# Two layers on one core: later groups convolve by four shifted products, and the long filter moves ahead of the inverse

## The chip, the core and the metric

The kernel is one program on one core of a Trainium2 chip. The metric is device time in microseconds (us) of one execution; of several runs the median is taken. A core has TensorE (PE; its weight loads are listed as PEld), VectorE (DVE), ScalarE (ACT), GpSimd (POOL) and SyncE (SP, which here issues every DMA). Each engine takes its instructions strictly in the order in which they stand in its queue.

## What is computed

Input x has 2 batches of 1024 rows of 128 features. Four blocks follow each other, each with a residual and a layer norm behind it: softmax attention with 8 heads, a gated feed-forward block with ternary weights (ffn0), a gated delta-rule attention on chunks of 32 rows (here L1), and a feed-forward block with weights of plus and minus one (ffn1). The change touches L1:

```python
q = silu(causal_dwconv(x @ Wq, conv_q))      # 4 taps, per channel; k and v alike
beta = sigmoid(x @ Wb)
q, k = l2norm(q), l2norm(k)                  # per head, in chunks of 32 rows
A = (k * beta) @ k.T
T = inv(eye + tril(A, -1))
u, w = T @ (v * beta), T @ (k * beta)
# scan over the chunks, state S of 32x32 per head
u_i = u_i - w_i @ S
o_i = q_i @ S + tril(q_i @ k_i.T) @ u_i
S = S + k_i.T @ u_i
local_short = causal_dwconv(v, fir_short)    # 3 taps
local_long = causal_dwconv(v, fir_long)      # 31 taps
o = w_global * o + (1 - w_global) * (p0 * v + p1 * local_short + p2 * local_long)
out = rmsnorm(o) @ Wo
```

## The kernel before

The 2048 rows are cut into four groups of 512 (`GROUPS`, line 60): 0 and 1 are the halves of batch 0, 2 and 3 those of batch 1. Group 1 needs from group 0, and 3 from 2, the last rows of projections and values and the scan's state S (`prev`, line 1443; copies on POOL such as L1122, L1240, L1248, L1406).

Four streams of instructions are written out (`PLAN`, line 54): one does ffn0 of groups 0 to 3 and then ffn1 of groups 0 to 3, on one set of buffers; one does L1 of groups 0 and 2, one L1 of group 1, one L1 of group 3. The attention (`pass1`, `pass2`) is written before all of them. Streams "b" and "c" (groups 1 and 3) are `late`: their buffers lie where the attention's lay, so they begin only after it, and some of their steps are written for DVE and ACT instead of POOL. Their PSUM banks (`BANKS`, line 52) are one for group 1 and two for group 3; the stream of groups 0 and 2 has one and gets a second for group 2.

The order on each engine is not that of the text. A planner in the file (`Plan`, lines 168 to 524) builds the graph of dependencies, gives every instruction a price, and simulates all engines. Among the instructions that are ready it takes the one with the best rank: a backward critical path less a bonus per step and group, from the table `AHEAD` (line 20), in us. `RUN` (line 18) holds three more: `switch` is a penalty for PE changing its tile shape; when PE's real work of the last window is under `target` columns and nothing is ready, the planner puts in a dummy product of constants (tile ip, line 1594, and a small form through L1066). The order found is then fixed by dependencies.

L1 of one group (`l1_attn`, line 1072) has these steps:

- l1prep: transposes of the group's rows into xT (L782, L1100), then `conv` for k. `conv` (line 1103) projects with one product of float32 128x512 (L1106), copies it behind three columns of the half before (ACT L1112, POOL L1109 or L1111), multiplies by the last tap (ACT L1115 in late groups, DVE L1117 in the others), adds three taps on DVE (L1119), takes tanh (ACT L1121); then (th+1)*a on DVE gives k (L1142), q (L1188) or v (L1238).
- l1gate: one product, then the gates; norms of k on POOL (L1131, L1133, a power) and beta (L1165 to L1182). Then `conv` for q.
- l1gram: small products of k with k and q (L1066), scaled by DVE (L1199 needs nbet, L1200).
- l1inv: the inverse of the two 16x16 blocks, 15 steps of two DVE instructions (L1214, L1215), in the tiles `nm` and `pr`; ACT or POOL scales (L1225, L1227), DVE transposes (L1228).
- l1v: `conv` for v, L1238, a transposed copy vC (L1246), products with beta (L1250, L1251).
- l1fir: the short filter on ACT, DVE or POOL; for the long one eight DMAs copy vC into two tiles of tag `pj` (L1277), eight DMAs bring 128 KB each of Toeplitz matrices into the tiles `nm` and `pr` in turn (L1282), and 128 small products follow (L1286), 16 for each of the eight loads; DVE takes the result (L1298). Late groups do this after l1v, groups 0 and 2 after the scan.
- l1T doubles the inverse's blocks (products, L1321, L1325), l1wu forms w, u and the scan's matrices, l1scan does 16 dependent steps (L1398 or L1066, L1401), l1out and l1rms finish (L1425 to L1441).

The tags decide the order of l1inv and l1fir: the matrices of the long filter use `nm` and `pr`, so they can be loaded only when the inverse has let go of them.

In front, `prep_rest` (line 709) splits the weights of ffn0 into two parts each and writes them back to HBM (L714, L718, L719); `norm_in` (line 788) loads one half of x into `xt`, normalises it (DVE for the first, POOL L776 for the second) and transposes it; `proj` fills `hi` and `lo`, which SP copies into the stacks (L862, L869).

The line numbers are those of the profile before.

Of the kernel before, what the change touches and what calls it, by code (L numbers as in the profile page):

```python
# [17 lines left out]
RUN = {'dummies': True, 'target': 4688, 'rewarm': False, 'switch': 282251}  # L18
TURNS = 5
AHEAD = {  # L20
    "ffn0": {"00": 33.9, "01": 19.1, "10": -42.8, "11": -632.3},
    "ffn1": {"00": -414.5, "01": 8.0, "10": 14.7, "11": 14.8},
    "l1T": {"00": -49.6, "01": 20.4, "10": -47.0, "11": -18.8},
    "l1fir": {"00": 34.9, "01": 73.7, "10": -3.2, "11": 151.3},
    "l1gate": {"00": 58.9, "01": 42.1, "10": 2.8, "11": 7.5},
    "l1gram": {"00": 143.6, "01": -110.1, "10": 30.9, "11": 98.4},
    "l1inv": {"00": -57.9, "01": 14.3, "10": 69.3, "11": 4.6},
    "l1out": {"00": -136.2, "01": -72.3, "10": -173.5, "11": 60.6},
    "l1prep": {"00": 13.3, "01": -18.5, "10": 28.2, "11": 119.7},
    "l1rms": {"00": 42.7, "01": -222.7, "10": 82.0, "11": 22.0},  # L30
    "l1scan": {"00": -5.2, "01": 75.8, "10": 102.9, "11": 103.9},
    "l1v": {"00": 34.4, "01": 4.4, "10": 11.7, "11": -8.4},
    "l1wu": {"00": 23.3, "01": -28.3, "10": 20.7, "11": -28.0},
    "norm_in": {"0": 303.2, "1": 23.6},
    "pass1": {"0": 29.5, "1": 252.9, "2": -5.4, "3": -11.7, "4": 23.4, "5": -36.2, "6": 62.4, "7": 23.3},
    "pass2": {"0": -31.7, "1": -116.1, "2": -18.2, "3": 37.7, "4": 31.5, "5": 146.2, "6": 75.2, "7": 6.1},
    "post": {"00": 118.3, "01": 180.9, "10": 872.1, "11": 572.6},
    "prep": {"": 42.3},
    "stacks": {"00": -46.3, "01": 58.4, "10": -93.7, "11": -15.8},
    "stk": {"0": 3.6, "1": -44.0, "2": 10.1, "3": -43.0, "4": -60.5, "5": 0.7, "6": -48.2, "7": -0.5},  # L40
    "weights": {"": 53.1},
}
HALVES, RU = 1, 1
O1, O2, O3, O4 = 0, 1, 1, 1
# [483 lines left out]
def body(ctx: ExitStack, tc: tile.TileContext, A, out, dbg=None):  # L528
# [3 lines left out]
    plan, early, alive = Plan(), set(), []  # L532

# [61 lines left out]
    eye16 = const.tile([128, 16, 16], F32, name="eye16")  # L595
    wd = dram.tile([14, 128, 2, 4, 128], F32R, name="wd")
# [112 lines left out]
    def prep_rest():  # L709

        mark("weights")
        for c in range(11):
            raw = FA.big.tile([128, 512], F32, tag="u", name="raw", bufs=2)
            nc.sync.dma_start(out=raw, in_=A["wf"][c])  # L714
            w = FA.big.tile([128, 2, 4, 128], F32R, tag="w", name="w", bufs=FA.wb)
            hi = w[:, 0].rearrange("p a b -> p (a b)")
            nc.scalar.copy(hi, raw)
            nc.gpsimd.tensor_tensor(w[:, 1].rearrange("p a b -> p (a b)"), raw, hi.bitcast(F32), ALU.subtract)  # L718
            nc.sync.dma_start(out=wd[c].bitcast(F32), in_=w.bitcast(F32))  # L719
# [15 lines left out]
        nc.sync.dma_start(out=eye16, in_=A["eye16"])  # L735
        ku4 = FA.big.tile([128, 7, 128], mybir.dt.uint32, tag="alo", name="ku4", bufs=2)
# [51 lines left out]
    def norm_in(b):  # L788

        mark(f"norm_in:{b}")  # L790
        xt = xp.tile([128, 8, 128], F32, tag="xt", name="xt")
# [168 lines left out]
    def mm3(p, whi, wlo, ahi, alo, nk):  # L960
        for k in range(nk):
            n = 0
            for w, a in ((whi, ahi), (wlo, ahi), (whi, alo)):
                nc.tensor.matmul(p, w(k), a(k), start=(k == 0 and n == 0), stop=(k == nk - 1 and n == 2))  # L964
                n += 1
# [15 lines left out]
    def ffn0(F, gi, late):  # L981
# [22 lines left out]
        for c0, cs in ((2, C_H1S), (6, C_H2S)):  # L1004
            nhi = t2048(F, "ahi")
# [66 lines left out]
    def l1_attn(L, gi, late):  # L1072
# [19 lines left out]
        def m(label):  # L1092
            mark(f"{label}:{b}{hg}")
# [5 lines left out]
        xT = own("xT", (128, 512))  # L1099
        nc.scalar.copy(xT, px)  # L1100
        h3 = halo("h3", (128, 3, 3))

        def conv(w, mi):

            p = bank(L, [128, 512])
            nc.tensor.matmul(p, mats[:, mi, :], xT, start=True, stop=True)  # L1106
            pj = own("pj", (128, 515), 2)
            if first:
                nc.gpsimd.memset(pj[:, 0:3], 0.0)  # L1109
            else:  # L1110
                nc.gpsimd.tensor_copy(pj[:, 0:3], pb["pj"][:, w, :])  # L1111
# [10 lines left out]
            nc.gpsimd.tensor_copy(h3[:, w, :], pj[:, 512:515])  # L1122
# [79 lines left out]
        m("l1inv")  # L1202

        xa = tmp("xa", C3)
        nc.vector.transpose(xa, flat(an).rearrange("p (b e) -> p e b", e=16))
        am = own("am", (128, 16, 16))
        nc.vector.tensor_scalar(am, xa[:, :, 0:16], sc(C_EV), None, ALU.mult)
        nc.vector.scalar_tensor_tensor(am, xa[:, :, 16:32], sc(C_OD), am, ALU.mult, ALU.add)
        nm = own("nm", (128, 16, 16))
        nc.gpsimd.tensor_copy(nm, eye16)  # L1210
        pr = own("pr", (128, 16, 16))
        for k in range(15):
            o = pr[:, 0:15 - k, 0:k + 1]
            nc.vector.tensor_tensor(o, bcast(am[:, k, k + 1:16], k + 1), nm[:, k:k + 1, 0:k + 1].to_broadcast([128, 15 - k, k + 1]), ALU.mult)  # L1214
            nc.vector.tensor_tensor(nm[:, k + 1:16, 0:k + 1], nm[:, k + 1:16, 0:k + 1], o, ALU.add)  # L1215
            if k % 5 == 4:
                yield 4.0
                m("l1inv")
        nB = own("nB", C3)
        tt = own("tt", C3)  # L1220
        for e, src, dst in ((side, nm, tt), (nc.gpsimd, nm.rearrange("p i k -> p k i"), nB)):
            xn = tmp("xn", C3)
            for i, c in ((0, C_EV), (16, C_OD)):
                if late and O3:
                    nc.scalar.activation(xn[:, :, i:i + 16], src, AF.Identity, scale=sc(c))  # L1225
                else:
                    e.tensor_scalar(xn[:, :, i:i + 16], src, sc(c), 0.0, ALU.mult, ALU.add)  # L1227
            nc.vector.transpose(flat(dst).rearrange("p (b e) -> p e b", e=16), xn)  # L1228
        yield 4.0
        m("l1v")  # L1230

        th, a = conv(2, M_LV)
        vT = own("v", (128, 514))
        if first:
            nc.gpsimd.memset(vT[:, 0:2], 0.0)
        else:
            nc.gpsimd.tensor_copy(vT[:, 0:2], pb["v"])
        nc.vector.scalar_tensor_tensor(vT[:, 2:514], th, 1.0, a, ALU.add, ALU.mult)  # L1238
        hv = halo("hv", (128, 2))
        nc.gpsimd.tensor_copy(hv, vT[:, 512:514])  # L1240
        vC = own("vC", (128, 17, 32))
        if first:
            nc.gpsimd.memset(vC[:, 0, :], 0.0)
        else:
            nc.gpsimd.tensor_copy(vC[:, 0, :], pb["vC"])
        nc.vector.transpose(flat(vC[:, 1:17, :]), vT[:, 2:514])  # L1246
        hvC = halo("hvC", (128, 32))
        nc.gpsimd.tensor_copy(hvC, vC[:, 16, :])  # L1248
        kv = own("kv", (128, 16, 64))
        nc.gpsimd.tensor_tensor(kv[:, :, 0:32], kC, bcast(betk, 32), ALU.mult)  # L1250
        side.tensor_tensor(kv[:, :, 32:64], vC[:, 1:17, :], bcast(bet, 32), ALU.mult)  # L1251
        yield 5.0

        def fir():
# [16 lines left out]

            pf = bank(L, [128, 32, 16])
            v2 = [own("pj", C3, 2) for hp in range(2)]
            for h in range(4):
                for j in range(2):
                    o = 64 * (h % 2) + 32 * j
                    nc.sync.dma_start(out=v2[h // 2][o:o + 32], in_=vC[32 * h:32 * h + 32, j:j + 16, :])  # L1277
            row = []
            for d in range(32):
                if d % 4 == 0:  # L1280
                    toep = own(("nm", "pr")[d // 4 % 2], (128, 2, 4, 32))
                    nc.sync.dma_start(out=toep, in_=A["toep"][d // 4])  # L1282
                for h in range(4):
                    g, e = divmod(h, 2)
                    s = slice(64 * e, 64 * e + 64)
                    row.append(nc.tensor.matmul(pf[32 * h:32 * h + 32, d, :], toep[s, g, d % 4, :], v2[g][s, :, d],  # L1286
                                                start=True, stop=True, tile_position=(64 * e, 32 * h)))
                if d % 4 == 3:
                    together(row)
                    row = []  # L1290
                if d == 15:
                    yield 4.0
                    m("l1fir")
            yield 4.0
            m("l1fir")
            nc.gpsimd.tensor_tensor(fsC, fsC, bcast(ge[:, :, 1], 32), ALU.mult)
            lC = own("xT", C3)
# [9 lines left out]
            nc.gpsimd.tensor_tensor(wgl, wgl, rq, ALU.mult)  # L1307
            yield 5.0
            return lC

        if late:
            lC = yield from fir()
            steps = [own("pj", (128, 4, 128), 2) for i in range(2)]
            for st in steps:
                nc.gpsimd.memset(st, 0.0)
# [381 lines left out]
```

## Time and profile before

| what | us |
|---|---|
| median of 3 runs | 618.89 (616.68, 618.89, 622.49) |
| the profiled execution, its own time | 621.76 |
| its span, first to last instruction | 620.0 |
| PE busy, mean granted clock | 572.1, 0.981 |
| DVE, ACT, POOL busy | 422.5, 338.6, 248.0 |
| dummy products on PE (L1594 alone) | 28.7 |
| DMA moved | 57.63 MB, 93 GB/s |

The page gives for each engine busy time, share of the span and instructions; then the span in 40 slices of 15.5 us, each digit the busy share in tenths, and under PEclk the clock that PE was granted. Windows give the same numbers for chosen stretches, for all work or for that of one tile. The chain of waits is followed back from the last instruction, at each step to what released it: "DMA nm<-toep" is a load of filter matrices for which the next product waited, "SPq L1277" the time in which SP issued copies.

The stages of the profiled execution: preparation to about 46 us; attention, with ffn0 of groups 0 and 1 and most of L1 of group 0 between, to 342; the rest of ffn0 (last product at 454.4); L1 of groups 1 to 3; ffn1 of group 0 from 460, of group 1 from 552, of group 2 from 575, of group 3 from 595.

### The profile page before, as it was taken

Reading aid. Unit: us, or ns where it says so; the run is one execution under the profiler, and the core shown is the slowest. Engines: PE = TensorE matmul, PEld = TensorE weight load, DVE = VectorE, ACT = ScalarE, POOL = GpSimd, SP = SyncE. Lnnn points to the kernel's source line nnn. Section 1 sums busy time; section 2 is a strip of 40 time slices with the busy share of each in tenths; the row PEclk is TensorE's granted clock in tenths of the full one; section 3 lists DMA queues with packets and bytes.
Section 4 is the critical chain, followed back from the end, with each engine's and each line's share of the span. In section 5 each row is a group of like instructions: output and inputs, shape, how many; then the busy total and the mean of one; then the engine's idle time right before and its main releaser. Section 6 shows DMA issues by size and latency. Waiting matters only on the chain.

```text
span 620.0 us, 18247 instructions
## 1 busy us (share of the span) xinstructions
PE 572.1 (92%) x7729; PEld 360.7 (58%) x7758; DVE 422.5 (68%) x994; ACT 338.6 (55%) x611; POOL 248.0 (40%) x343
## 2 busy tenths in 40 slices
PE   4889999999999999999999989987989998799984
PEld 2264455567665556666556656664666655567653
DVE  5957888884736799498742266885588788374763
ACT  3676456764868884886887562352444523125331
POOL 6886021221303426023691561567514832561210
PEclk9979999999999999999999999999799999999997
DMA  8697520216131323213112433252313203202220
GB/s 258 202 287 267 121 40 2 42 44 176 45 103 55 65 69 119 69 35 121 29 44 71 129 111 104 89 172 69 136 39 80 80 21 94 68 6 70 86 86 17
DMA packets 26595, 57.63 MB, mean 93 GB/s; under 512 B 4049, under 2 KB 12881, under 8 KB 26514
## 3 DMA queue, kind: packets, MB, share of 16 engines
q1 hardware_dynamic: 26514, 56.47, 30.3%
q8 instruction: 61, 1.00, 0.7%
q14 instruction: 20, 0.16, 0.1%
HBM read 40.40 MB, written 8.39 MB: 79 GB/s over the span
## 4 chain that ended last, share of the span: by engine, by line
PE 70%; DVE 10%; DMA 8%; ACT 5%; issue 3%; POOL 2%; SPq 2%; POOLq 0%; ACTq 0%; DVEq 0%
PE ps L964 17%; PE pv L931 10%; PE s L924 10%; PE ps L884 9%; PE ps L1066 7%; PE ps L1449 3%; PE ps L1450 3%; DMA nm<-toep 3%; DMA raw<-wf 3%; SPq L1277 1%; PE ip L1594 1%; PE ps L1286 1%; DVE cv L1119 1%; PE ps L1106 1%; PE ps L782 1%
## 5 line engine op out<-in xcount | busy, mean ns | idle before, releaser
L886 DVE TENSOR_REDUCE mp<-ps 128x1 f32<-128x512 f32 x224 | 140.4, 682 | 47.6 <-PE ps L884 47.0
L926 ACT ACTIVATE p<-s 128x512 f32<-128x512 f32 x236 | 131.1, 600 | 47.4 <-PE s L924 34.3
L964 PE MATMUL ps<-ahi,w 128*128 128x512 f32 x352 | 124.0, 416 | 2.6 <-ACT u L1017 2.4
L924 PE MATMUL s<-q,k 128*128 128x512 f32 x236 | 92.0, 422 | 0.2 <-ACT p L926 0.2
L884 PE MATMUL ps<-k,q 128*128 128x512 f32 x240 | 87.8, 424 | 2.9 <-DVE m L892 1.1
L964 PEld LDWEIGHTS ps<-ahi,w 128*128 128x128 f32 x352 | 65.1, 192 | 23.8 <-ACT p L926 3.4
L931 PE MATMUL pv<-p,va 128*32 128x512 f32 x512 | 72.0, 601 | 0.0
L964 PE MATMUL ps<-alo,w 128*128 128x512 f32 x176 | 71.7, 408 | 0.2 <-POOL alo L979 0.2
L884 PEld LDWEIGHTS ps<-k,q 128*128 128x128 f32 x240 | 43.8, 190 | 34.8 <-DVE mp L886 17.8
L924 PEld LDWEIGHTS s<-q,k 128*128 128x128 f32 x236 | 42.8, 189 | 25.4 <-ACT p L926 14.4
L1449 PE MATMUL ps<-ahi,w 128*128 128x512 f32 x96 | 39.8, 414 | 2.4 <-DVE alo L1465 2.0
L1001 POOL TENSOR_TENSOR alo<-u,ahi 128x512 fp32r<-128x512 f32 x16 | 20.7, 1291 | 52.4 <-ACT ahi L1000 46.0
L1450 PE MATMUL ps<-alo,w 128*128 128x512 f32 x96 | 39.5, 412 | 1.0 <-DVE alo L1465 0.7
L964 PEld LDWEIGHTS ps<-alo,w 128*128 128x128 f32 x176 | 33.7, 192 | 8.8 <-POOL alo L979 0.8
L1464 ACT ACTIVATE ahi<-ps 128x512 fp32r<-128x512 f32 x32 | 18.7, 597 | 27.8 <-PE ps L1450 27.6
L1119 DVE SCALAR_TENSOR_TENSOR cv<-pj,cvh,cv 128x512 f32<-128x512 f32 x36 | 30.6, 851 | 4.3 <-ACT cv L1115 4.0
L1465 DVE SCALAR_TENSOR_TENSOR alo<-ps,ahi 128x512 fp32r<-128x512 f32 x32 | 21.6, 687 | 16.7 <-ACT ahi L1464 16.6
L1594 PE MATMUL ip<-rest 128*128 128x512 bf16 x110 | 28.7, 379 | 2.4 <-issue 1.9
L931 PEld LDWEIGHTS pv<-p,va 128*32 128x32 f32 x512 | 13.3, 108 | 29.2 <-issue 27.2
L859 POOL MEMSET q<- 2x1024 f32 x5 | 4.8, 950 | 63.2 <-issue 37.0
L1401 DVE TENSOR_TENSOR tt<-ps,an 128x32 f32<-128x32 f32 x64 | 11.7, 185 | 25.6 <-PE ps L1066 19.3
L766 POOL TENSOR_SCALAR r<-mv 128x4 f32<-128x4 f32 (+1 forms) x24 | 6.3, 261 | 44.8 <-DVE mv L764 39.8
(264 smaller groups left out, 1061.9 us busy)
## 6 DMA issues: line engine op xcount, KB each, us to landing
w<-wd SPq DMA_DIRECT2D x56, 512.0 KB, 3.4
wd<-w SPq DMA_DIRECT2D x14, 512.0 KB, 4.2
raw<-wf SPq DMA_DIRECT2D x11, 256.0 KB, 3.1
pr<-toep SPq DMA_DIRECT2D x16, 128.0 KB, 3.0
nm<-toep SPq DMA_DIRECT2D x16, 128.0 KB, 3.1
pj<-vC SPq DMA_DIRECT2D x32, 64.0 KB, 2.0
q<-hi SPq DMA_DIRECT2D x14, 128.0 KB, 2.3
k<-hi SPq DMA_DIRECT2D x28, 64.0 KB, 2.4
```

The lines of the kernel that those rows point to most:

```text
L884: nc.tensor.matmul(p, q[:, s * 128:(s + 1) * 128], d, start=True, stop=True)
L886: nc.vector.tensor_reduce(mp[:, s, e, i:i + 1], p, AX.X, ALU.max)
L924: nc.tensor.matmul(s2, ks[e][:, t * 128:(t + 1) * 128], q[:, i * 512:(i + 1) * 512], start=True, stop=True)
L926: nc.scalar.activation(p, s2, AF.Exp, scale=0.25)
L931: together([nc.tensor.matmul(pv[32 * j:32 * j + 32, :], va[:, t - 1, 2 * pr + j % 2, :], pend[j % len(pend)], start=(t == 1), stop=(t == 8 ...
L964: nc.tensor.matmul(p, w(k), a(k), start=(k == 0 and n == 0), stop=(k == nk - 1 and n == 2))
L1066: r.append(nc.tensor.matmul(p(hs), lhsT(hs), rhs(hs), start=True, stop=True, tile_position=(32 * h, 32 * h)))
L1119: nc.vector.scalar_tensor_tensor(a, pj[:, t:t + 512], cvh[:, 4 * w + t:4 * w + t + 1], a, ALU.mult, ALU.add)
L1449: nc.tensor.matmul(p, w(k), ahi(k), start=(k == 0), stop=False)
L1450: nc.tensor.matmul(p, w(k), alo(k), start=False, stop=(k == nk - 1))
L1465: nc.vector.scalar_tensor_tensor(lo, p, 0.0, hi.bitcast(F32), ALU.max, ALU.subtract)
L1594: order[n] = Op(nc.tensor.matmul(ip, rest[:, 0:128], rest, start=True, stop=True).ins, 0)
```

## The change

For groups 1, 2 and 3 (`CVG = 1`) projection and convolution become four float32 products that accumulate in one bank, each with the weight matrix times one tap (`wc`, made in `prep_rest`: a broadcast load of the taps, one scaling, three multiplies on POOL) and a view of xT shifted by one column. xT gets three columns in front, zero or copied from the half before. Tanh reads the bank, and the step behind reads tanh and the bank. Group 0 convolves as before.

The matrices of the long filter in groups 1 and 3 get a pool of five tiles of their own (`TR = 5`). In these groups l1v and the long filter are written before l1inv (`FE = 1`), and the short filter and the sum stay behind it; the planner still chooses the order.

`xt` shares the buffer of `hi` (`XH = 1`); `mm3` and the split of the weights are the same as before (`ZLO = 0`). ffn0 and ffn1 are marked in three parts each, so that `AHEAD` has more rows; all its numbers are new, `target` goes from 4688 to 3863 and `switch` from 282251 to 95802.

```diff
-RUN = {'dummies': True, 'target': 4688, 'rewarm': False, 'switch': 282251}
+RUN = {'dummies': True, 'target': 3863, 'rewarm': False, 'switch': 95802}
...
-    "l1fir": {"00": 34.9, "01": 73.7, "10": -3.2, "11": 151.3},
-    "l1inv": {"00": -57.9, "01": 14.3, "10": 69.3, "11": 4.6},
-    "l1prep": {"00": 13.3, "01": -18.5, "10": 28.2, "11": 119.7},
+    "l1fir": {"00": 76.3, "01": -58.9, "10": -81.4, "11": -84.8},
+    "l1inv": {"00": 101.8, "01": 124.4, "10": 110.0, "11": 21.8},
+    "l1prep": {"00": 10.8, "01": 11.3, "10": -147.9, "11": -216.2},
...
+ZLO, CVG, XH, TR, FE = 0, 1, 1, 5, 1
...
+        if wc is not None:
+            nc.sync.dma_start(out=wc, in_=A["cw"].to_broadcast([128, 1536]).rearrange("p (w t c) -> p w t c", w=3, t=4))
+            half = FA.big.tile([128, 3, 128], F32, tag="u", name="half", bufs=2)
+            nc.gpsimd.tensor_scalar(half, mats[:, 0:3, :], 0.5, 0.0, ALU.mult, ALU.add)
+            for w in range(3):
+                nc.gpsimd.tensor_tensor(wc[:, w], wc[:, w], half[:, w:w + 1, :].to_broadcast([128, 4, 128]), ALU.mult)
...
-        xt = xp.tile([128, 8, 128], F32, tag="xt", name="xt")
+        xt = xp.tile([128, 8, 128], F32, tag="hi" if XH else "xt", name="xt")
...
-        xT = own("xT", (128, 512))
+        xTh = own("xT", (128, 515))
+        xT = xTh[:, 3:515]
...
         def conv(w, mi):
             p = bank(L, [128, 512])
+            if gi >= CVG:
+                for t in range(4):
+                    nc.tensor.matmul(p, wc[:, w, t, :], xTh[:, t:t + 512], start=t == 0, stop=t == 3)
+                th = tmp("th")
+                nc.scalar.activation(th, p, AF.Tanh)
+                return th, p
...
-                    toep = own(("nm", "pr")[d // 4 % 2], (128, 2, 4, 32))
+                    toep = own(("nm", "pr")[d // 4 % 2], (128, 2, 4, 32)) if tpool is None or gi not in (1, 3) else tpool.tile([128, 2, 4, 32], F32, tag="toep", name="toep", bufs=TR)
...
+        if late and FE:
+            vT, vC, hv, hvC, kv = yield from values_()
+            lC = yield from fir_long()
+            nB, tt = yield from inverse()
+        else:
+            nB, tt = yield from inverse()
+            vT, vC, hv, hvC, kv = yield from values_()
+            lC = None
         if late:
-            lC = yield from fir()
+            lC = yield from fir(lC)
...
+    if TR:
+        tpool = pool("toepp", 1, None, ctx, reuse_waits="tile")
```

## Prediction

> **What bounds the kernel now.** I read the page first: busy shares, the 40 slices with the granted clock, the chain that ended last; then the windows of the stretch after the attention, once for all engines and once for the dummy products alone (tile ip), then the chain and the timeline around group 3.
>
> ```profile
> PE 572.1 (92%) x7729; PEld 360.7 (58%) x7758; DVE 422.5 (68%) x994; ACT 338.6 (55%) x611; POOL 248.0 (40%) x343
> PE   4889999999999999999999989987989998799984
> PEclk9979999999999999999999999999799999999997
> PE 70%; DVE 10%; DMA 8%; ACT 5%; issue 3%; POOL 2%; SPq 2%; POOLq 0%; ACTq 0%; DVEq 0%
> ...
> L1119 DVE SCALAR_TENSOR_TENSOR cv<-pj,cvh,cv 128x512 f32<-128x512 f32 x36 | 30.6, 851 | 4.3 <-ACT cv L1115 4.0
> L1594 PE MATMUL ip<-rest 128*128 128x512 bf16 x110 | 28.7, 379 | 2.4 <-issue 1.9
> ```
>
> TensorE (PE) looks like the bound everywhere, at 92%. But the share mixes two stages, and L1594 is work without use: products of constants that the planner puts in where nothing is ready. Up to 342 us (last attention products) the PE row is full with real work. Behind it:
>
> ```profile
> 342.00:454.00 112.00, 101.36 (x1722) 68.53 (x1723) 70.94 (x163) 48.15 (x79) 59.04 (x83) 0.95 0.36 112
> 454.00:545.00 91.00, 81.67 (x2806) 55.09 (x2822) 67.81 (x196) 30.63 (x64) 41.79 (x59) 1.00 0.23 65
> 545.00:620.00 75.00, 61.41 (x977) 45.19 (x972) 43.13 (x129) 25.27 (x52) 18.00 (x22) 0.96 0.17 54
> ```
> ```profile
> 342.00:454.00 112.00, 8.28 (x52) 0.95 0.36 112
> 454.00:545.00 91.00, 24.00 (x173) 1.00 0.23 65
> 545.00:620.00 75.00, 8.12 (x41) 0.96 0.17 54
> ```
>
> First fence: length, busy PE, weight loads, DVE, ACT, POOL, then granted clock. Second: the part of PE that is dummies. Idle plus dummies is 10.6+8.3=18.9, 9.3+24.0=33.3 and 13.6+8.1=21.7 us: 73.9 of 278 us are free. So after 342 the end is set by a chain, and the chain of waits says which:
>
> ```profile
> 517.17 0.55 DVE cv L1119
> ...
> 522.30 0.58 SPq L1277
> ...
> 527.14 3.31 DMA pj<-vC
> 530.50 0.45 PE ps L1286 x27
> 530.97 3.71 DMA nm<-toep
> 534.72 0.52 PE ps L1286 x33
> 535.24 2.84 DMA nm<-toep
> 538.12 0.52 PE ps L1286 x33
> 538.63 3.08 DMA nm<-toep
> ```
>
> This is the last group (3). Its inverse ends at 517.2 (last transpose, L1228); then value convolution, eight copies of vC, and the long filter in rounds: load two matrices, two short sets of products, load again. No arithmetic engine is the limit here.
>
> **Part 1, one set of shifted products (groups 1, 2, 3; nine convolutions).** Removed: 27 L1119 at 0.851 us = 23.0, and 3 L1117 at 0.745 = 2.2 on DVE; 9 L1112 at 0.591 and 6 L1115 at 0.685 = 9.4 on ACT; some 18 POOL copies and memsets at about 0.2 = 3.6. Added: 27 products. One L1106 product is two records, and the chain prices such a pair at 0.86 us: 23.2 us of PE, 7.7 per group. Their weight loads (0.19 each) run beside PE.
>
> Groups 1 and 2 convolve between 354 and 449: +15.5 us where 18.9 us are free. Two stalls of that stretch should go with Part 3 and the freed DVE. At 421.9-432.0 PE ran 1.9 us of filter products and 4.8 of dummies while ffn0 of group 3 waited; its input was written by DVE L979 at 425.7, its product came at 432.2, behind the filter in PE's order: 6.5 us. Then the clock halves; by its means in 3.4 us windows (the last but two of the columns below) from 432.7 to 442.9, 10.2 us, 5.1 lost:
>
> ```profile
> 426.90:430.30 3.40, 2.25 (x70) 1.29 (x71) 0.30 (x1) 0.00 (x0) 2.93 (x1) 1.00 0.31 80
> 430.30:433.70 3.40, 1.87 (x67) 1.33 (x68) 0.00 (x1) 0.96 (x2) 0.04 (x1) 0.85 0.03 6
> 433.70:437.10 3.40, 3.40 (x15) 2.02 (x15) 3.40 (x7) 1.46 (x4) 2.90 (x6) 0.50 0.82 306
> ```
>
> Net +15.5-6.5-5.1=+4 us; ends -11 (all added work fits the free time) and +15.5 (no stall goes). I take +4: the stretch had only 16% free, nearer to full than to empty.
>
> For group 3 the products are on the path. Its k product started at 475.4 and its gram inputs were complete at 500.5 (L1188): 25.1 us, mostly DVE queueing (the L1119 of q ran at 491.3-494.0, the L1188 waited until 499.2). Now 3.44 for k, 0.86 gate, 3.44 for q, tanh 0.64, L1188 1.04, hand-overs 0.5: 9.9 us. But L1199 also needs nbet, which POOL wrote at 492.1 behind a 2.9 us power; k comes 3.7 us earlier (480.1 instead of 483.8), so 488.4. L1199 moves from 501.8 to 488.4 at best, 13 us. I take -7, half, since scans and ffn1 still hold DVE at 75% in 454-545; ends 0 and -13.
>
> A new wait: the product's bank is now held until th and it are combined, so tanh 0.64 and 0.7 to 1.0 of DVE, instead of two ACT copies (0.59+0.69). Group 1 has one bank; its next product (gate, gram) waits at the head of PE's in-order queue, everything behind it too. About 0.2 to 1.5 us for each of 3; in the ends above.
>
> Group 3 also waited for its input: L776 began at 464.7, the other three ran at 471.8, behind group 2's convolution and value work. 3.0 us of it vanish: -2 (0 to -7).
>
> **Part 2, preparation and buffers in front.** A broadcast load of 768 KB: 512 KB took 3.4 us, 448 KB 6.5, so 5 to 10 us of queue q1; on POOL one scale (0.69 for 128x512, L1267) and three multiplies (1.32, L718): 4.6 us. All in the first 60 us, where DMA runs at 0.97 in 40-50. It delays the copies wd<-w; their first readers are the L969 at 57.4 and L964 at 120.4, so 60 us of cover: 0, or +5 to +10 if it weren't there. The second half of x moves into a buffer that SP's group 1 stacks (L862, L869) last read at 83.4. Its two loads were issued at 12.6, past all of those; now after them. Landing 3.0, statistics 2.2, power 1.0, eight L776 on POOL at 0.8: ready at about 100; the transposes ran at 113.8. 0, with 14 us to spare (POOL 24% busy in 46-120); late, it would hold up group 2's stacks (118.5) and cost PE up to 10. The first 40 us lose 6.4 us of POOL work for the 4.6 gained: 0.
>
> **Part 3, filter before the inverse, five buffers (groups 1, 3).** Between 517.2 and the end of the block doubling (L1325, 546.7) lie 29.5 us. Group 2 did the same step, from its last transpose (469.1) to L1325 (479.5), in 10.4. So 19.1 us go. What moves ahead of the inverse on DVE: L1238 0.69, L1246 0.70, L1251 1.1, L1298 0.69: +3. Net -16; ends -20 and -5 (if PE, in order, still waits for matrices in front of T). All 16 DMA issues of a group (8 of 0.59, 8 of 0.33: 7.4 us) go past the inverse on SP; before, the loads could start only when the inverse had let go of nm and pr. Now the inverse's 13.7 us of DVE (503.5 to 517.2) cover 5 issues, a landing of 2.0 and 4 us of products. Late next: the loads six to eight still reuse a buffer (3.0 each). SP holds ffn0's weights (L969) behind a blocked load; before, two came right after the last one at 432.7.
>
> **Part 4, ranks, switch, target.** They change the order on every engine and the number of dummies; no row prices them. Up to 342 PE is full, so order has little to give there. Bounds -5 and +12 (half of the 24 us of dummies of the middle stretch); I take 0.
>
> **Sum.** +4-7-2-16 = -21 us. Against the profiled execution: span 620.0 to 599.0, with its 1.8 us outside 600.8 instead of 621.8. That execution is 2.9 above the median of 618.9; the same step there gives **598 us**.
>
> **A rule against a row.** The clock fell after a stretch whose longest PE gap was 1.9 us, with 1.9 to 2.7 of each 3.4 us busy. The Trainium skill, "TensorE: Matmul & The Clock Gate" (Part 1), says that the clock halves after an idle window of about 3.4 us. By the rule there was no such window, the half clock would have another cause and stay, and the sum would be -16 and the time 603; by the row it goes with the filter's waits.
>
> **Rivals.**
> *A, group 2 becomes last.* Its filter keeps two buffers, after its scan (511.4 to 523.5). ffn1 runs group by group on one set of buffers. Group 2's input was ready at 558.4 (POOL L776), its ffn1 takes 20 (574.8 to 594.7), group 3's another 25 from its transposes (595.05) to the end: 603, so 602 as a median. For it: ffn1 of group 2 ended right before group 3's. Against it: group 2's output products (526 to 539) were interleaved with group 3's filter waits, which go. If group 1 is also not earlier (its ffn1 551.6 to 574.8), nothing is gained: 619.
> *B, PE takes the added products in full.* +15.5 instead of +4: -9.5, 609. For it: 99% PE up to 342 and dense patches behind; against it: 73.9 us free.
> *C, the clock (slower).* The target for dummies falls from 4688 to 3863, so fewer are put in; a stretch on fir or scan at 60 to 75% PE drops to half clock as at 433. Each us at half clock costs 0.5: 42 us eat the 21, 55 make it 1% slower; 70 would give 633. Against it: 520-545 was as thin and kept 1.00, and the added products fill thin places.
> *D, the new order misses on the chip*: a load late in SP's order with PE behind it, as now (18.0 us of L1282 waiting for L1286), and the filter's wait merely moves before the inverse: Part 3 gives -5 to 0 and B holds: 618 to 623.
>
> **Chances.** Forecast 0.60 (582 to 611); A 0.17, of it 0.05 with nothing gained; B 0.10, half of it within 1% with less from DVE; C 0.11; D 0.02. Faster by over 1% (about what a measurement can tell): 0.60+0.12+0.05=0.77; within 1%: 0.05+0.05+0.02=0.12; slower 0.11. The ends added outright (-11-13-7-20-5=-56) don't all occur, since real PE work after 342 (204 us) plus 23 plus the last ffn1's 14 us of gaps already give 583. The range of 584 to 621 leaves out C and some 0.08 below and between.
>
> **What would show it.** Right: about 27 more pairs of products, nine L1119 left (group 0), toep loads issued before the inverse's first L1214, no toep waits in front of PE for groups 1 and 3, T within 11 us of the inverse's end, the dummies well under 28.7 us, clock 1.0 around group 1's filter. Wrong: half clock over more than 20 us after 342; ffn0 of group 3 ending past 458 with PE full; ffn1 of group 2 ending later than 580; a gap in the PE row around 115 (second half of x).

## The result and the profile after

The kernel after takes 621.96 us (median of 20 runs, 617.68 to 627.76), the kernel before beside it 618.77 (20 runs). The ratio, taken from the executions that did not fall into the chip's slower state, is 1.0069 with a 95% interval of 1.0049 to 1.0089: 4 us slower, where 21 us of gain were forecast. The profiled execution took 623.41 us, its span 621.6.

Part of the 4 us goes with PE's granted clock. Beside the experiments the kernel before was run in five more sets, 64 executions; the median clock of a set was 0.987 to 0.991. The ten executions with a clock of 0.977 to 0.983 took 622.0 us in the mean, and the profiled one (621.76 us, 0.981) is like them. The median clock of the kernel after is 0.982; its ten executions in the same band took 623.0 us. At equal clock the two kernels are 1 us apart.

The page of the kernel after: PE's total, the PE and clock rows, the shares of the chain, and the group of the new products.

```profile
PE 573.3 (92%) x7588; PEld 361.0 (58%) x7588; DVE 399.4 (64%) x964; ACT 334.6 (54%) x600; POOL 241.8 (39%) x331
PE   4979999999999999999989999989998998898884
...
PEclk9969999999999999999899999999999998999998
...
PE 78%; DVE 6%; DMA 5%; ACT 4%; POOL 4%; issue 3%; SPq 1%; POOLq 0%; DVEq 0%; ACTq 0%
...
L1133 PE MATMUL ps<-xT,wc 128*128 128x512 f32 x72 | 34.4, 599 | 0.0
```

The work changed as forecast: 36 products (72 records) replace 9, DVE falls by 23 us, and the clock dip at 433 is gone. The filter's DMA waits left the chain (DMA 8% to 5%). Yet PE is as busy as before. The windows of the three late stretches, for all engines and then for the dummies alone, say why:

```profile
342.00:454.00 112.00, 106.93 (x1961) 70.73 (x1959) 59.64 (x165) 55.11 (x87) 50.49 (x72) 1.00 0.34 109
454.00:545.00 91.00, 83.84 (x2566) 58.02 (x2558) 56.68 (x170) 30.58 (x64) 38.12 (x55) 0.98 0.22 66
545.00:620.00 75.00, 59.24 (x815) 40.72 (x813) 39.92 (x118) 21.54 (x44) 20.30 (x22) 0.97 0.18 57
```
```profile
342.00:454.00 112.00, 1.60 (x5) 1.00 0.34 109
454.00:545.00 91.00, 7.98 (x29) 0.98 0.22 66
545.00:620.00 75.00, 10.81 (x37) 0.97 0.18 57
```

Dummies fell from 40.4 to 20.4 us; the products take room that they had, and the lower `target` asks for fewer (the two were not told apart). Idle plus dummies went from 73.9 to 48.4 us: from 18.9 to 6.7 in the first stretch, from 33.3 to 15.1 in the second, and from 21.7 up to 26.6 in the third.

Group 3's path became shorter, as forecast. DVE's end of its inverse and the end of the block doubling (L1373), kernel after:

```profile
529.60 1.05 DVE L1257 STREAM_TRANSPOSE tt<-xn 128x512 f32<-128x512 f32 x1 [1.04 <-ACT xn L1254]
530.84 1.05 DVE L1257 STREAM_TRANSPOSE nB<-xn 128x512 f32<-128x512 f32 x1 [0.19 <-ACT xn L1254]
...
540.48 0.41 DVE L1373 TENSOR_TENSOR tt<-tt,ps 128x256 f32<-128x256 f32 x1
```

9.0 us lie between them, where 29.5 did. From the last transposes of ffn0 of group 3 to the input of its ffn1, the path takes 115.0 us (477.7 to 592.7), before 138.1 (457.3 to 595.4): 23.1 us gained.

In this trace the gain is gone in two places. First, that path begins 20.4 us later. Second, group 2 became a wall. Either alone holds the end near the old one: by its late start group 3 gets to ffn1 only 2.7 us earlier, and the wall stands at 596.2, behind the 595.05 at which these transposes began before. PE's timeline at the last two rounds of group 2's filter, SyncE's at their last load, then the chain of waits from there (start, us, what), all of the kernel after:

```profile
531.74 0.38 PE L1305 MATMUL ps<-pj,pr 64*32 64x16 f32 x23 [0.68 <-issue]
...
557.99 0.45 PE L1305 MATMUL ps<-pj,nm 64*32 64x16 f32 x32
558.26 0.47 PE L1305 MATMUL ps<-pj,pr 64*32 64x16 f32 x32
```
```profile
532.18 0.33 SPq L1301 DMA_DIRECT2D pr<-toep  x1
```
```profile
560.43 1.25 POOL xT L1339
561.75 1.28 POOL xT L1342
...
565.51 2.92 POOL rs L1483
...
570.05 1.14 PE ps L1489 x8
...
574.97 3.67 POOL x L791 x4
...
579.04 0.70 ACT ahi L1506
...
595.50 0.70 ACT u L1058
596.24 0.65 PE ps L797 x4
```

The last matrices were issued at 532.2 (in the kernel before such a load landed in 3 us), but their products stand at 558.0 in PE's order. So group 2's sum, norm and input of ffn1 come at 578.6 instead of 558.4; its ffn1 ends at 595.5, and the transposes for ffn1 of group 3 (596.24) wait for it, though that input was ready at 592.7.

### The profile page after: what moved, and what is told of

It reads as the page before. It is cut to its first block, busy times and chain, and to the rows that moved or that the text cites. A ratio compares the mean times of both kernels' runs of the same rounds, so it can differ in the third digit from the quotient of the medians.

```text
span 621.6 us, 17876 instructions
## 1 busy us (share of the span) xinstructions
PE 573.3 (92%) x7588; PEld 361.0 (58%) x7588; DVE 399.4 (64%) x964; ACT 334.6 (54%) x600; POOL 241.8 (39%) x331
## 4 chain that ended last, share of the span: by engine, by line
PE 78%; DVE 6%; DMA 5%; ACT 4%; POOL 4%; issue 3%; SPq 1%; POOLq 0%; DVEq 0%; ACTq 0%
PE ps L979 21%; PE pv L946 10%; PE s L939 9%; PE ps L899 9%; PE ps L1082 7%; PE ps L1133 5%; PE ps L1498 3%; PE ps L1497 3%; DMA raw<-wf 2%; PE ps L1305 1%; DVE alo L1513 1%; DMA w<-wd 1%; PE ip L1646 1%; PE ps L797 1%; PE ps L676 1%
## 5 line engine op out<-in xcount | busy, mean ns | idle before, releaser
L899 PE MATMUL ps<-k,q 128*128 128x512 f32 x240 | 89.5, 427 | 3.3 <-DVE m L907 1.2
L979 PEld LDWEIGHTS ps<-ahi,w 128*128 128x128 f32 x352 | 63.5, 189 | 25.5 <-issue 4.5
L1512 ACT ACTIVATE ahi<-ps 128x512 fp32r<-128x512 f32 x32 | 18.6, 596 | 40.7 <-PE ps L1498 38.5
L1133 PE MATMUL ps<-xT,wc 128*128 128x512 f32 x72 | 34.4, 599 | 0.0
L1513 DVE SCALAR_TENSOR_TENSOR alo<-ps,ahi 128x512 fp32r<-128x512 f32 x32 | 21.5, 686 | 17.7 <-ACT ahi L1512 17.6
L993 POOL TENSOR_TENSOR alo<-z,ahi 128x512 fp32r<-128x512 f32 x8 | 10.2, 1292 | 53.4 <-PE s L939 40.9
L1497 PEld LDWEIGHTS ps<-ahi,w 128*128 128x128 f32 x96 | 18.4, 192 | 11.3 <-DVE alo L1513 5.7
```

The costliest lines, as they stand in the source:

```text
L899: nc.tensor.matmul(p, q[:, s * 128:(s + 1) * 128], d, start=True, stop=True)
L1133: nc.tensor.matmul(p, wc[:, w, t, :], xTh[:, t:t + 512], start=t == 0, stop=t == 3)
L1497: nc.tensor.matmul(p, w(k), ahi(k), start=(k == 0), stop=False)
L1513: nc.vector.scalar_tensor_tensor(lo, p, 0.0, hi.bitcast(F32), ALU.max, ALU.subtract)
```

## The experiments

All times below are ratios to the kernel before on the same chip; "us" is the ratio less 1, times 618.8.

| run | ratio, 95% interval | us |
|---|---|---|
| kernel after | 1.0069 (1.0049 to 1.0089) | +4.3 |
| products cut, groups 1 and 2 | 0.9981 (0.9947 to 1.0015) | -1.2 |
| products cut, all | 0.9885 (0.9827 to 0.9943) | -7.1 |
| products for group 3 only, planned anew | 1.0330 (1.0265 to 1.0395) | +20.4 |
| old parts, new ranks | 1.0380 (1.0320 to 1.0439) | +23.5 |
| ffn0 of group 3 ahead by 60 | 1.0187 (1.0140 to 1.0235) | +11.6 |
| ffn0 of group 3 ahead by 250 | 1.0328 (1.0284 to 1.0371) | +20.3 |
| filter part, old ranks | 1.0289 (1.0247 to 1.0331) | +17.9 |
| all parts, old ranks | 1.0347 (1.0304 to 1.0391) | +21.5 |
| after's order: products in group 3 only | 1.0100 (1.0063 to 1.0136) | +6.2 |
| after's order: filter behind the inverse | 1.0302 (1.0256 to 1.0348) | +18.7 |
| after's order: no products | 0.9985 (0.9950 to 1.0020) | -0.9 |
| before's order: products | 1.0300 (1.0255 to 1.0345) | +18.6 |
| before's order: filter of group 3 | 1.0121 (1.0067 to 1.0175) | +7.5 |
| before's order: both | 1.0184 (1.0106 to 1.0261) | +11.4 |
| before's order: products in group 3 | 1.0229 (1.0156 to 1.0302) | +14.2 |
| before's order: products cut | 1.0271 (1.0208 to 1.0334) | +16.8 |
| filter part, own order | 1.0020 (0.9988 to 1.0052) | +1.2 |
| all parts, own order | 0.9955 (0.9921 to 0.9989) | -2.8 |

Seven runs came outside every range that was stated for them before: products cut in all groups (612.7 us), products for group 3 only planned anew (639.5), all parts with old ranks (640.4), after's order with products in group 3 only (625.2), and before's order with the filter (626.5), with both (629.2) and with products in group 3 (633.0). Four of these miss the nearest range by 0.4 to 1.2 us, the first, second and fifth by 2.7, 15.5 and 4.5.

**First theory: PE's time.** The added products fill 356 to 476 and push ffn0 of group 3 back. The cut kernels keep every engine's order (the planner still prices 512 columns) and make three of four products six columns wide:

```diff
-                    nc.tensor.matmul(p, wc[:, w, t, :], xTh[:, t:t + 512], start=t == 0, stop=t == 3)
+                    n = 6 if t and gi < 3 else 512
+                    nc.tensor.matmul(p[:, 0:n], wc[:, w, t, :], xTh[:, t:t + n], start=t == 0, stop=t == 3)
```

> The kernel after, in the same order on every engine, but three of the four products of each convolution of groups 1 and 2 are 6 columns wide instead of 512 (three taps are left out there, so the output is another one). 18 products of about 0.9 us, 16 us of PE, go out of the stretch 342 to 476. Theory (PE has no time to give in that stretch, and what the products take there is handed on to the end of ffn0 of group 3): the last product of ffn0 of group 3 ends at 460 or before instead of 476, group 3's x is ready by 473 instead of 487, and the time is 605 to 612. Rival 1 (the new order, not the products, is what puts ffn0 of group 3 late and holds the end): 618 to 623. Rival 2 (group 2's chain, with the last pair of its long filter at 558, sets the end whatever group 3 does): ffn0 of group 3 earlier, but 616 to 622.

> As the run with groups 1 and 2 cut, and group 3's nine products cut too (three taps are left out in all late groups): another 8 us of PE, between 488 and 512, where PE mostly waits. Theory: little beyond the run with groups 1 and 2 cut alone, 1 to 4 us less, as k, q and the gram that waits for them come some us earlier: 602 to 610. Rivals 1 and 2: 616 to 622.

Cutting groups 1 and 2 took 12.2 us of PE (the products' 22.1 us became 9.9) and gave 5.5 us: 618.1 us, where the rivals had been put and not the theory. The last transposes of ffn0 of group 3 came at 473.6, 4.1 earlier, with the same 144 us behind. Group 3's nine more gave another 6, more than expected. So by the cuts the products' time costs some 11 us, and 16 of the 20.4 us by which the path starts late did not go with them. But a part of the freed time went into a lower clock where PE had been thinned out. Windows of the kernel after, then of this one (length, PE, PEld, DVE, ACT, POOL, clock):

```profile
380.00:420.00 40.00, 37.53 (x854) 25.93 (x845) 27.16 (x71) 14.53 (x24) 19.64 (x26) 1.00 0.40 126
420.00:454.00 34.00, 32.61 (x761) 20.77 (x759) 24.75 (x71) 16.98 (x30) 19.70 (x29) 1.00 0.23 72
```
```profile
380.00:420.00 40.00, 35.96 (x876) 25.73 (x877) 28.11 (x83) 13.74 (x23) 19.54 (x30) 0.96 0.36 115
420.00:454.00 34.00, 30.52 (x776) 21.42 (x774) 24.32 (x61) 16.27 (x31) 19.77 (x28) 0.90 0.21 69
```

0.04 of 40 and 0.10 of 34 us are 5.0 us of clock, so the products' time may cost some us more than the cuts show.

**One part undone, planned anew.** Products for group 3 only, or all parts as before with the ranks of after; the copies for the halos are put back where they are needed.

```diff
-ZLO, CVG, XH, TR, FE = 0, 1, 1, 5, 1
+ZLO, CVG, XH, TR, FE = 0, 3, 1, 5, 1
```
```diff
-ZLO, CVG, XH, TR, FE = 0, 1, 1, 5, 1
+ZLO, CVG, XH, TR, FE = 0, 4, 0, 0, 0
```

> Products for group 3's convolutions only; groups 1 and 2 go back to one product and the scalar and vector taps, and the output is the reference's; everything else as in the kernel after, its ranks too. Theory: PE has 15.5 us less to do between 342 and 476, so ffn0 of group 3 ends by 462 and the time is 605 to 613, faster than both kernels. Rival 1 (order): 618 to 624. Rival 2 (group 2's chain): its filter's last pair still near 555 and the time 616 to 622.

> Only the new ranks: projection and taps, the buffers and the place of the filter as before, with the ranks of the kernel after. Theory: ffn0 of group 3 ends by 460 as before, and the 20 us of the filter after the inverse come back: 613 to 625. Rival 1 (the new order is what costs): ffn0 of group 3 ends at 470 or later with no added products, and 628 or more.

Both are 20 us or more slower than the kernel before, with less or nothing of the change. Here ffn0 of group 3 ended early: its last transposes came at 472 and 430 instead of 478. In the second run the time of its rival came (628 or more), but not the rival's condition (ffn0 of group 3 at 470 or later). The first theory falls, and so does the view that this moment sets the end.

**Second theory: PE's order in front of ffn0 of group 3.** 1324 of the 2176 small products stand ahead of its end in the kernel after, 864 before.

```diff
-    "ffn0": {"00": 70.2, "01": 70.7, "10": -27.9, "11": -34.3},
-    "ffn0b": {"00": 36.8, "01": 16.3, "10": -33.1, "11": -174.1},
-    "ffn0c": {"00": 12.1, "01": 53.3, "10": 4.2, "11": -252.9},
+    "ffn0": {"00": 70.2, "01": 70.7, "10": -27.9, "11": 25.7},
+    "ffn0b": {"00": 36.8, "01": 16.3, "10": -33.1, "11": -114.1},
+    "ffn0c": {"00": 12.1, "01": 53.3, "10": 4.2, "11": -192.9},
```

> The kernel after with one thing changed: the three ranks of ffn0 of group 3 are 60 higher, so that 832 of the 2176 small products of the scans stand before its end in PE's order instead of 1324 (864 in the kernel before); the 30 products of convolutions ahead of it stay. The first theory has fallen to a quarter: cutting 18 of the 24 products ahead of it brought its end forward by 4 us only. Second theory: what stands ahead of ffn0 of group 3 in PE's written order, with the waits of those scans, holds it. Then its end comes at 460 to 468 instead of 478, and with the tail of 136 us of the kernel after behind it the time is 606 to 616. Rival (group 2's chain ends with group 3's and takes over): its last ffn1 is later by what its scan was put back, and the time is 619 to 632.

> As the run with ranks 60 higher, but 250 higher: 640 small products and 18 of convolutions ahead of the end of ffn0 of group 3, 12 products of group 2's convolutions behind it. Second theory: end of ffn0 of group 3 at 450 to 458; 600 to 612. Rival (group 2's chain takes over): 622 to 640, with ffn1 of group 2 the last to get its input.

ffn0 of group 3 did end earlier (453 and 441), the time grew. In the run with 60, DVE's norm of that result, with POOL's power between (460.05, 1.04), reads:

```profile
457.26 0.36 DVE L779 BATCH_NORM_AGGREGATE mv<-st 128x2 f32<-128x6 f32 x4
...
473.06 0.34 DVE L791 TENSOR_SCALAR x<-u,mv,r 128x128 f32<-128x128 f32 x1
...
478.50 0.81 DVE L791 TENSOR_SCALAR x<-u,mv,r 128x128 f32<-128x128 f32 x2
479.64 0.34 DVE L791 TENSOR_SCALAR x<-u,mv,r 128x128 f32<-128x128 f32 x1
```

All it needed was there at 461.1; it ran 12 to 18 us later, behind other groups' work in DVE's order. The time won on one engine was given back on the next. In the run with 250 the rival holds: group 2 got its input of ffn1 last (transposes at 594.0), and those of group 3 (613.9) followed only behind that ffn1. This theory, as a single place, falls too.

The other way round, the ranks of before (`RUN` and `AHEAD`, one row each for ffn0 and ffn1) under the filter's part (`CVG = 4`) or under all parts:

> The ranks of the kernel before and its projections and taps; of the change only the filter ahead of the inverse with its own buffers and the layer input in the large buffer. The prediction's term for this part alone was -16: 600 to 606 if nothing else moves. Rival (a planned order follows its ranks and its program together, and a part put into ranks that were set for another program costs more than the part brings, as the new ranks on the old structure cost 23 us): 625 to 645.

> All parts of the change with the ranks of the kernel before (ffn0 and ffn1 keep one rank for their three stages). By the prediction's sum 598 to 604; by the second theory 1428 small products stand before the end of ffn0 of group 3, more than in the kernel after, so its end comes at 478 or later and the time is 620 to 640.

With the ranks of before, one part or all parts cost 18 to 22 us: the rival of the first run holds.

**Third theory: the order as a whole.** The order was found for one set of parts; to price a part, the order must be held. So the positions of one kernel's plan were written down per step, engine and tile, and used as ranks (no `switch`); an instruction that stays is to keep its place, a new one takes that of its neighbour in the step. The planner still takes what is ready, so an order is held only in part (numbers below), and neither order was run in this way with all its own parts unchanged.

```diff
-    plan.run(rank, least=WARM, **RUN)
+    plan.run(ranks.get, least=WARM, **dict(RUN, switch=0))   # ranks: start of each instruction in the other plan
```

In the order of after, with `CVG, XH, TR, FE` of 3, 1, 5, 1, of 1, 1, 0, 0 and of 4, 0, 5, 1:

> The order of the kernel after is written down and used as the ranks, so that instructions that stay keep their places; groups 1 and 2 go back to one product and three taps each, group 3 keeps its products, and the filter stays ahead of the inverse. This is the run with products for group 3 only, without its new order. Theory now (products of groups 1 and 2 bring or cost 4 us at most; the 640 of the earlier run was its order): 614 to 624. First theory (PE's time between 342 and 476): 602 to 612. Rival (the taps that come back on VectorE, about 30 instructions of 0.6 us, hold group 3's norm as in the earlier run): 630 to 642.

> The order of the kernel after as ranks, all its products; only the filter of groups 1 and 3 goes back behind the inverse, with the two buffers of before for its matrices. What this run is above the kernel after is the worth of the filter's move in its order. The prediction had 16 us: 634 to 642. Rival (group 2's chain ends with group 3's, so that the filter is hidden): 620 to 628.

> The order of the kernel after as ranks, the filter ahead of the inverse with its own buffers, no products of shifted columns in any group, and the layer input in its old buffer. If the products of all three groups bring little, as the cut runs say: 616 to 626. If VectorE's taps hold group 3 (about 9 more instructions of 0.6 us on its path, 7 us in the prediction, and as many in groups 1 and 2 ahead of it): 626 to 640. If PE's time decides: 605 to 614.

Filter back behind the inverse: 14.4 us more than the kernel after (18.7 less 4.3), with 25.6 us between inverse and block doubling. The prediction had 16. Two more things moved in that run: the last transposes of ffn0 of group 3 came at 450.4 instead of 477.7, yet group 3's inverse began at the same 513.5; and behind 545 the mean clock was 0.79 instead of 0.97, so a part of the 14.4 is clock. No products at all (and the layer input in its old buffer): 5.2 us less. Products in groups 1 and 2 undone: 1.9 more, inside the intervals. The 639 of the first such run had been its order. The run without products and the one with group 3's alone together say that group 3's products, with that buffer, cost 7.1 us in this order (6.2 less -0.9), although they make its path shorter.

In the order of before (`XH = 0`; the products' weights are laid out after the attention; the filter is moved in group 3 only, by its ranks and this line):

```diff
-        if late and FE:
+        if late and FE and gi == 3:
```

> The order of the kernel before as ranks and the filter as before; only the convolutions of groups 1, 2 and 3 become products of shifted columns (their weights are laid out once attention's buffers are free, instead of at the start). The prediction's sum for this part: +4 for groups 1 and 2, -7 and -2 for group 3, so 613 to 619. If the products take their full 23 us of PE on the way to the end: 630 to 642. Between, 622 to 630, if half of them lies beside waits.

> The order of the kernel before as ranks, its projections and taps; only group 3's filter goes ahead of the inverse with five buffers (its loads 18 us before the inverse, its products and the value convolution ahead of the inverse's first instruction). If the parts add (15 us for the move, whatever the convolutions are): 600 to 606, faster than both kernels. If the move pays only where the products made group 3's chain the last (group 2's chain and ffn1 of group 2, which ended at 595 in the kernel before, hold the end): 614 to 622.

> The order of the kernel before as ranks, products in groups 1 to 3 and group 3's filter ahead of the inverse. If the parts add: 637 less 15, 619 to 625, as the kernel after. If the move's worth depends on the order of after: 630 to 640.

> The order of the kernel before as ranks, the filter as before; products in group 3 only. The prediction had -9 for them. In the run with products in all three groups group 3's inverse began 7 us later than before, not 7 earlier, with the end of ffn0 of group 3 where it was: if group 3's own products carry that, 625 to 632 here; if the products of groups 1 and 2 carry it (their work and group 1's later scans lie in PE's way at 475 to 515), 612 to 621.

> As the run with products in groups 1 to 3 in the order of before, the same order on every engine, but three of four products of each convolution are 6 columns wide (three taps are left out, so the output is another one): about 24 us of PE less. If PE's time for the products is what costs: 612 to 622, 15 to 25 us less than the 637 of the run with whole products. If the order that the products forced, or the dummies and the clock, is what costs: 628 to 637.

Here the products cost 18.6 us, and cutting them to six columns gives back only 2. That does not clear PE's time: the cut takes the products from 36.0 to 15.8 us of PE, but the clock falls as well, from 0.981 to 0.989 in the four executions with whole products to 0.953 to 0.969 (in 420 to 454, 1.00 to 0.75). 0.025 of 635 us is some 16 us, as an estimate: about what the cut could have brought. The run leaves PE's time and the order both open.

The filter's move alone costs 7.5; on top of the products it gains 7.2. The move alone did not shorten the way from the inverse to the block doubling to 9 us: 23.9 us lie between them (525.2 to 549.1), 27.2 with the products. PE's timeline in the run with the move alone shows why. It has the first products of the doubling (tt<-..an) behind rounds of group 2's filter, which still waits for its two buffers nm and pr:

```profile
532.83 0.45 PE L1347 MATMUL ps<-pj,nm 64*32 64x16 f32 x32 [0.44 <-DMA nm<-toep]
...
540.56 0.65 PE L1119 MATMUL ps<-tt,an 32*32 32x16 f32 x55
```

In the order of after the doubling stands ahead of the last pair of group 2's filter: group 3 gains, and group 2's pair comes at 558. The two chains ask for the same place in PE's order.

The products of group 3 alone cost 14.2. In that run the first rows of group 2's scan and of its filter, before and with the products of group 3:

```profile
495.29 0.41 PE L1398 MATMUL ps<-tt,pj 128*128 128x32 f32 x2 [0.19 <-DVE au L1377]
...
511.43 0.72 PE L1286 MATMUL ps<-pj,nm 64*32 64x16 f32 x31
```
```profile
502.92 0.41 PE L1463 MATMUL ps<-tt,pj 128*128 128x32 f32 x2
...
520.38 0.81 PE L1322 MATMUL ps<-pj,nm 64*32 64x16 f32 x31
```

Group 2 has no product in this kernel, yet its scan starts 7.6 us later and its filter 9.0. Group 3's q products ran at 491 to 495, ahead of that scan, and its v products at 505 to 511, between the scan's dependent steps; that they hold it is argued, not shown. In the run with the products cut (in all groups) the filter still began at 519.85, but at a clock of 0.74 in 500 to 520 (0.83 with whole products), so it does not tell their length from the clock.

**Own orders.** Two sets of parts got ranks searched by the kernel's own planner, for as long each: the filter's part alone (`CVG, XH, TR, FE` of 4, 0, 5, 1), and all parts.

> The filter of groups 1 and 3 ahead of the inverse with its own buffers, convolutions and the layer input's buffer as in the kernel before, and ranks searched for this set of parts by the kernel's own planner. If the order decides and the products bring nothing: 604 to 612, faster than both kernels and within 5 us of the other run. If the filter's move is worth nothing without products (the run with after's order, 617.7): 615 to 622.

> All parts of the change as in the kernel after, with ranks searched for as long from its own. If the order decides: 606 to 614. If the products cost PE time that no order hides: 616 to 624 here, while the run without products falls to 612 or less.

All parts with other ranks take 616.79 us, 0.9955 (0.9921 to 0.9989) of the kernel before and 7.0 us less than the kernel after: faster than both by a little, by ranks alone, though not by the 606 to 614 expected. This order lies close to that of after (ffn0's last transposes of group 3 at 474.3 instead of 477.7). Here the last pair of group 2's filter ran at

```profile
538.19 0.57 PE L1303 MATMUL ps<-pj,pr 64*32 64x16 f32 x32
```

20 us earlier than in the kernel after; group 2's ffn1 began at 566, and the transposes for ffn1 of group 3 at 587.2 instead of 596.2, and they waited for their own input (587.9), no longer for group 2. Of the 9.0 us there, 3.5 are the wall gone (in the kernel after that input had been ready at 592.7), the rest is group 3's own path. The 616 to 624 of the other reading came too, but not its condition: without products an own order reached only 620.92 instead of 612 or less, in the range of "the filter's move is worth nothing without products": with an order for them, the products seem to be worth some 4 us (0.9955 against 1.0020).

## Why the prediction was wrong

- **Part 1, groups 1 and 2 (+4).** Small, as said, but the sign is open: by the cut their time costs 5.5 us, and against the old taps, in after's order, they bring 1.9 (inside the intervals). The stall at 432 and the half clock went, as said (clock 0.85 to 1.00 in 420 to 454). But the 5.1 us for the clock were read from an execution at 0.981, and the median clock of the others is 0.987 to 0.991: so 0.007 of 620 us, 4.3 as an estimate, was probably not there to gain in a median execution, from which the forecast of 598 counts.
- **Part 1, group 3 (-7 and -2).** From its input to the inverse's start 26.3 us instead of 30.7: -4.4. From ffn0's transposes to the input 9.5 instead of 16.6: -7.1. The path shortened by about the sum; the time did not. In after's order group 3's products, with the layer input's buffer, cost 7.1 us, in the order of before 14.2. Part 1 as a whole had -5 in the sum and measured +5.2 in after's order: a shorter path of group 3 was taken for a shorter time.
- **Part 2 (0).** Nothing shows near 115; PE was busy 99.4 of 100 us from 100 to 200.
- **Part 3 (-16).** Right: inverse to block doubling -20.5, the inverse itself +5.8 (12.6 to 18.4) with more between its steps; 14.4 us by the run that undoes it, some of it clock. In the order of before the lower end (-5, "if PE, in order, still waits for matrices in front of T") is near what the move gained on top of the products (7.2), with group 2's matrices.
- **Part 4 (0): the step that failed.** It said "Up to 342 PE is full, so order has little to give there" and took 0 between -5 and +12. The attention ended 14.6 us later. Some 5.5 of that is ffn0 work done earlier (324 records instead of 300 by then, 0.23 each) and some 2 are small products of group 0's L1, but in 300 to 342 PE was busy 39.3 of 42 us at a clock of 0.96 where it had been 42.0 at 1.00, and in the first 100 us 85.2 instead of 87.1. Behind it, 460 more small products went ahead of ffn0 of group 3, whose path started 20.4 us late. That this start alone took back the 23.1 is not shown: the runs that brought it 24 to 36 us forward (453, 441, 450) were no faster. What is shown is the wall, which group 2's place in PE's order makes, and the spread: the same parts ran between 616.8 and 640.4 us by ranks alone, so the bounds for Part 4 were about -5 and +18 around the time measured, and the term could not be left at 0.
- **Rival A** gave 0.05 to the end that came: group 2 last and nothing gained (619). Its mechanism was another: not the two buffers, but 22 us in PE's order after the matrices had been there. The prediction took ffn1 of group 2 as ready at 558.4, a number of the old order; it became 578.6. ffn1 of group 2 ended right before that of group 3 began in the kernel before (594.7 and 595.05): two chains of equal length, so a gain on one alone was worth nothing. The prediction saw this pair and still gave the rival only 0.17. ffn1 was free for group 2 early enough (group 1's ended at about 566); group 2's own input was late.
- **B** is wrong for groups 1 and 2 (5.5 us by the cut, not 15.5). **C** is not refuted by the two profiled executions (0.982 against 0.981): against the other executions of the kernel before the clock is lower by 0.005 to 0.009, an estimated 3 to 6 us. Its direction was right; the 42 us at half clock that it names were not seen. **D** named 618 to 623, but for a load late in SP's order; the loads were in time here, PE's order was late.

Measured in after's order, the parts bring -14.4 for the filter and +5.2 for the products. With a total of +4.3 that leaves about +13 for the order, if the parts add; this is a remainder and not a measurement, since the old parts in exactly that order were not run, and in before's order the parts do not add. What stays open is whether an order exists in which the 23 us of group 3 come out; the best found brings 2.8. Which wait in before's order makes the products cost 18.6 stays open too; the late scan and filter of group 2 are seen in one run, their cause is argued.

## What to carry to other kernels

Where a planner writes the order, a change of the program and its ranks is a new program: hold the order and move one part, or search an order for each variant, before a part is called good or bad. Before adding up savings on one chain, look for the next chain that ends within the saving, and for the shared stage behind both (here ffn1, 17 to 20 us for group 2, one group after the other). A term for "new order" belongs in the range with the spread that other orders of the same program show. A stall or a half clock read from one profile is worth its size only if the other executions have it too.

## What the hardware showed beyond that

- The clock halved after a window that was busy for 60%, not idle. PE windows of the kernel after (length, busy, clock), with a longest gap of 1.35 us in the second:

```profile
509.90:513.30 3.40, 3.40 (x119) 1.00 0.03 8
513.30:516.70 3.40, 2.05 (x133) 1.00 0.41 111
516.70:520.10 3.40, 3.40 (x73) 0.52 0.36 88
```

The Trainium skill, "TensorE: Matmul & The Clock Gate" (Part 1), speaks of an idle window of about 3.4 us; here as before the change no such window came first. That agrees with the prediction's reading by the row, but a busy share alone does not decide it. In the same execution 533.8 to 537.2 was busy for 2.18 us and 578.1 to 581.5 for 2.24, and the clock stayed at 1.00 behind both; it fell to 0.53 in 301.6 to 305.0 behind a window that was busy for 2.87. What decides is not shown.
- A product six columns wide is not free: 36 such records kept PE busy for 4.5 us, 0.125 each, with a weight load of 0.19 beside each, against 0.46 for 512 columns (22.1 us for 48).
